# A recurrence over image columns: sigmoid of z into PSUM, running maximum by halves, and program order on every engine

## The chip, the cores and the metric

The kernel runs on one core of a Trainium2 chip. The core has a tensor engine (PE), a vector engine (VectorE, DVE in the profile), a scalar engine (ScalarE, ACT), GpSimd (POOL) and SyncE (SP), which here only issues DMA transfers. Each engine works through its own queue of instructions in order and waits on semaphores for the others. The metric is the device time of one execution in microseconds (us); lower is better. All data is float32.

## What is computed

The input x has shape (8, 32, 256, 256): batch, channel, row, column. Four layers follow one another, each as x + layer(groupnorm(x)): a Fourier layer, a 5x5 convolution, a recurrence over the columns, and a layer of running maxima in four directions with a 1x1 mix. The change touches the third layer. Cut to what matters, it is:

```python
def _cell(prev_col, cur_col, ...):          # both (batch, row, channel)
    x = concatenate([prev_col one row up, prev_col, prev_col one row down], axis=-1)
    i_vals = einsum('bhk,ok->bho', x, weight_ih) + bias_ih
    h_vals = einsum('bhc,oc->bho', cur_col, weight_hh) + bias_hh
    r = sigmoid(r_i + r_h); z = sigmoid(z_i + z_h)
    n = tanh(n_i + r * n_h)
    return n * z + cur_col * (1.0 - z)
# new_col of column w is prev_col of column w + 1; 255 such steps one after another
```

The fourth layer needs, among others, the running maximum of the third layer's result (with its residual added) from the first column to the last. That maximum is taken along the way, in the recurrence, since its columns come out in that order.

## The kernel before

The kernel has four stages: `forward_and_mix` and `inverse_and_conv` for the first two layers, `recurrence` for the third, `maxima_and_mix` for the fourth. They hand data on through DRAM: `x2d` into the recurrence, `x3d` (its result) and `fwd` (the running maximum) out of it.

In `recurrence` the 128 partitions are 4 residues of the row times 32 channels; the free axes are batch (8), column and 64 rows. Columns come in blocks of 8 (`WB`), 32 blocks (`NB`). Within a column the batch is worked on in two halves of 4 images (`NC`, index x), so that one half's matmuls can run while the other half's activations do. One step n = 2 w + x is one half of one column; a block has 16 steps. A step's tiles are 128 x 256.

One step consists of these parts (line numbers of before):

- `main` (L686): three matmuls of 128x128 weights for the gates r, z and ni, on the previous state `hs` of the same half.
- `cross` and `own` (both by L660): 32x32 matmuls, four at a time. `cross` adds the neighbours that `main` leaves out; `own` computes ahead for the NEXT step the part that depends on the current column alone (r, z and nh).
- L728: r = sigmoid on ScalarE. L729: VectorE (nh + bias) * r. L730: + ni.
- L731: z = sigmoid. L732: zm = 1 - z as a sigmoid of the negated value. L733: tanh.
- L735: GpSimd a = zm * current column. L737: VectorE n * z. L738: + a, which is the new state `hs`.
- L739: GpSimd adds the new state into the raw block `xw`, which becomes the layer's output.

Beside the steps there are: the load of a block from `x2d` (L645, 2 MB, four buffers), its normalisation on ScalarE (L653, eight activations of 128x512 a block into `xn`), the running maximum `fm` on VectorE (L763, one 128x512 per column, both halves at once), eight `bn_stats` a block (L775) for the next layer's statistics, and the stores of `x3d` and `fwd` (L752, eight transfers of 256 KB for each in every block).

The order in which an engine meets this work comes from two sources. Outside `manual_schedule` a scheduler orders instructions by their data and priorities; it may move a load far ahead. `keep_in_program_order` pins single instructions to where the code has them. The running maximum and the `bn_stats` are put in a list, and `late()` takes one of them in every step, between L730 and L737:

```python
                nc.gpsimd.tensor_tensor(a, zm, cur, ALU.mult)
                late()
                nc.vector.tensor_tensor(m, m, z, ALU.mult)
```

[...] Four tags for each half (r, z, ni, nh) take one bank each; [...]

Of the kernel before, what the change touches and what calls it, by code (L numbers as in the profile page):

```python
# [9 lines left out]
F32 = mybir.dt.float32  # L10
AF = mybir.ActivationFunctionType
ALU = mybir.AluOpType
# [4 lines left out]
P = 128  # L17
B, C, H, W = 8, 32, 256, 256
# [4 lines left out]
AFTER = mybir.DependencyInfo(mybir.DependencyClass.Sync, mybir.DependencyReason.DATA)  # L23
A = 4
Q = H // A
# [550 lines left out]
def recurrence(tc, k, d, x2d, x3d, fwd, stb, mean1, mv3):  # L576
# [4 lines left out]
    nc = tc.nc  # L581
    WB = 8
    NB = W // WB
    NH = 4
    NC = 2
    BC = B // NC
    with ExitStack() as ctx:
        one = ctx.enter_context(tc.tile_pool(name="bc", bufs=1))
        blk = ctx.enter_context(tc.tile_pool(name="bb", bufs=2))
        wk = ctx.enter_context(tc.tile_pool(name="bw", bufs=2))  # L590
        ps = ctx.enter_context(tc.tile_pool(name="bp", bufs=1, space=PSUM))

        def rows(i):
            return slice(32 * i, 32 * i + 32)
# [6 lines left out]
        for i in range(A):  # L601
            nc.sync.dma_start(out=wih[rows(i)], in_=d["wihT"].rearrange("(t c) (g o) -> c t g o", t=3, g=3))
            nc.sync.dma_start(out=whh[rows(i)], in_=d["whhT"].rearrange("c (g o) -> c g o", g=3))
            for j in range(A):
                if abs(i - j) < 2 and (i, j) not in ((1, 2), (2, 1)):
                    t = i - j + 1
                    nc.sync.dma_start(
                        out=wmain[rows(i), :, rows(j)],
# [3 lines left out]
        bhh = one.tile([P, 3], F32, name="bhh")  # L612
        nc.sync.dma_start(out=bih, in_=d["bih"])
        nc.sync.dma_start(out=bhh, in_=d["bhh"])
        brz = one.tile([P, 3], F32, name="brz")
# [23 lines left out]
        bst = one.tile([P, B, NB, 6], F32, name="bst")  # L639

        raws, norms, psums = {}, {}, {}

        def load(bi):
            t = blk.tile([P, B, WB, Q], F32, name=f"xw_{bi}", tag="xw", bufs=4)
            nc.sync.dma_start(  # L645
                out=t.rearrange("p b w q -> p b (w q)"),
                in_=x2d[:, :, :, bi * WB : (bi + 1) * WB, :].rearrange("b a c w q -> (a c) b (w q)"),
            )
            raws[bi] = t
            norms[bi] = blk.tile([P, B, WB, Q], F32, name=f"xn_{bi}", tag="xn")  # L650

        def normalise(bi, b):
            ins = nc.scalar.activation(  # L653
                norms[bi][:, b], raws[bi][:, b], AF.Identity, bias=shift[:, b : b + 1], scale=sc[:, 1, b : b + 1]
            )
            if bi:
                tc.keep_in_program_order(ins)

        def mm(out, i, j, lhsT, rhs, start, stop):
            return nc.tensor.matmul(out[rows(j)], lhsT=lhsT, rhs=rhs[rows(i)], start=start, stop=stop)  # L660

        R, Z, N = 0, 1, 2
# [4 lines left out]
        def own(n, gate):  # L667

            w, x = divmod(n, NC)
            if w >= W:  # L670
                return
            key = ("r", "z", "nh")[gate]
            out = psums[n, key] = ps.tile([P, BC, Q], F32, name=f"{key}_{n}", tag=f"{key}{x}")
            cur = norms[w // WB][:, x * BC : (x + 1) * BC, w % WB, :]
            for i in range(A):
                mm(out, i, i, whh[rows(i), gate, :], cur, True, gate == N)

        sem = tc.alloc_semaphore("own_parts")
        sigz = {}

        def main(n, prev):

            for gate, key in GATES:
                if gate == N:
                    psums[n, key] = ps.tile([P, BC, Q], F32, name=f"ni_{n}", tag=f"ni{n % NC}")
                nc.tensor.matmul(  # L686
                    psums[n, key], lhsT=wmain[:, gate, :], rhs=prev[:, :, 1 : 1 + Q], start=gate == N, stop=False
                )

        def cross(n, prev):  # L690

            for gate, key in GATES:
                if gate == Z:
                    own(n + 1, gate)
                for t, i, j, q0 in CROSS:
                    ins = mm(psums[n, key], i, j, wih[rows(i), t, gate, :], prev[:, :, q0 : q0 + Q], False, True)
                    if (gate, i) == (R, 3):
                        if n == NC:  # L700
                            ins._wait_ge(sem, 1)
                        else:
                            tc.add_manual_dep(ins.ins, sigz.pop(n - 1).ins.name, AFTER, reason="row groups of a bank")
                if gate != Z:
                    own(n + 1, gate)

        def step(w, x):
            bi, wi = w // WB, w % WB
            bs = slice(x * BC, (x + 1) * BC)
            raw, cur = raws[bi][:, bs, wi, :], norms[bi][:, bs, wi, :]  # L710
            new = hs[x][w % NH][:, :, 1 : 1 + Q]
            if w == 0:
                nc.vector.tensor_copy(new, cur)
            else:
                n, prev = NC * w + x, hs[x][(w - 1) % NH]
                if n == NC:
                    for gate in (R, Z, N):
                        own(n, gate)
                    tc.keep_in_program_order(nc.tensor.drain().then_inc(sem, 1))
                main(n, prev)  # L720
                cross(n, prev)
                p = {g: psums.pop((NC * w + x, g)) for g in ("r", "z", "ni", "nh")}
                r = wk.tile([P, BC, Q], F32, name=f"rs_{w}_{x}", tag=f"rs{x}")
                z = wk.tile([P, BC, Q], F32, name=f"zs_{w}_{x}", tag=f"zs{x}")
                m = wk.tile([P, BC, Q], F32, name=f"n_{w}_{x}", tag=f"n{x}")
                zm = wk.tile([P, BC, Q], F32, name=f"zm_{w}_{x}", tag=f"zm{x}")
                a = wk.tile([P, BC, Q], F32, name=f"a_{w}_{x}", tag=f"a{x}")
                nc.scalar.activation(r, p["r"], AF.Sigmoid, bias=brz[:, 0:1])  # L728
                nc.vector.scalar_tensor_tensor(m, p["nh"], bhh[:, 2:3], r, ALU.add, ALU.mult)  # L729
                nc.vector.tensor_tensor(m, p["ni"], m, ALU.add)  # L730
                sigz[n] = nc.scalar.activation(z, p["z"], AF.Sigmoid, bias=brz[:, 1:2])  # L731
                nc.scalar.activation(zm, p["z"], AF.Sigmoid, bias=brz[:, 2:3], scale=-1.0)  # L732
                nc.scalar.activation(m, m, AF.Tanh, bias=bih[:, 2:3])  # L733

                nc.gpsimd.tensor_tensor(a, zm, cur, ALU.mult)  # L735
                late()
                nc.vector.tensor_tensor(m, m, z, ALU.mult)  # L737
                nc.vector.tensor_tensor(new, m, a, ALU.add)  # L738
            nc.gpsimd.tensor_tensor(raw, raw, new, ALU.add)  # L739


        pieces, tops = [], {}

        def late():
            if pieces:
                tc.keep_in_program_order(pieces.pop(0)())

        def store(bi, dst, t):

            for a in range(A):  # L750
                for b2 in range(2):
                    nc.sync.dma_start(  # L752
                        out=dst[bi, :, b2, a].rearrange("(i c) n -> c i n", c=C),
                        in_=t[rows(a), 4 * b2 : 4 * b2 + 4].rearrange("p i w q -> p i (w q)"),
                    )

        def running(bi, wi):
            def piece():
                if wi == 0:
                    tops[bi] = blk.tile([P, B, WB, Q], F32, name=f"fm_{bi}", tag="fm", bufs=3)  # L760
                t, x = tops[bi], raws[bi][:, :, wi]
                last = t[:, :, wi - 1] if wi else tops[bi - 1][:, :, WB - 1] if bi else x
                ins = nc.vector.tensor_tensor(t[:, :, wi], x, last, ALU.max)  # L763
                if wi == WB - 1:
                    store(bi, fwd, t)
                return ins

            pieces.append(piece)

        def finish(bi):  # L770
            raw = raws[bi]
            store(bi, x3d, raw)
            for b in range(B):
                pieces.append(
                    lambda b=b: nc.vector.bn_stats(bst[:, b, bi, :], raw[:, b].rearrange("p w q -> p (w q)"))  # L775
                )

        load(0)
        for b in range(B):
            normalise(0, b)  # L780
        for bi in range(NB):
            if bi + 1 < NB:
                load(bi + 1)
            for wi in range(WB):
                for x in range(NC):
                    step(bi * WB + wi, x)
                running(bi, wi)
                if bi + 1 < NB and wi < WB // 2:
                    for b in (2 * wi, 2 * wi + 1):
                        normalise(bi + 1, b)  # L790
            finish(bi)
        while pieces:
            late()
        for b in range(B):
            nc.vector.bn_aggr(mv3[:, b, :], bst[:, b])

# [266 lines left out]
```

## Time and profile before

The time before is 3496.8 us, the median of 3 runs (3491.6 to 3498.0). The profiled execution spans 3489.2 us with a mean granted TensorE clock of 0.941.

| What | Value |
|---|---|
| PE busy | 3125.8 us, 90% of the span |
| VectorE busy | 2590.4 us, 74% |
| ScalarE busy | 1810.0 us, 52% |
| GpSimd busy | 883.8 us, 25% |
| L763 fm, 255 times | 289.7 us busy, mean 1136 ns |
| L739 raw add on GpSimd, 512 times | 349.8 us busy, mean 683 ns |
| L735 a on GpSimd, 510 times | 392.5 us busy, mean 770 ns |
| recurrence, 1262 to 2780 us | PE busy 1508.8 of 1518 us, VectorE 1286.7, ScalarE 1076.4, GpSimd 741.2 |
| DMA in that stretch | share 0.51, 130 GB/s |

In the groups of the page a row gives the line, engine and operation, the tiles written and read, the count, then the time busy in all and the mean of one, and last how long the engine was idle just before and who ended that wait. Busy time is an average over stages; what a change is worth in one stage is read from the waits of that stage. A busy PE isn't a PE at its peak.

### The profile page before, as it was taken

Reading aid. Unit: us, or ns where it says so; the run is one execution under the profiler, and the core shown is the slowest. Engines: PE = TensorE matmul, PEld = TensorE weight load, DVE = VectorE, ACT = ScalarE, POOL = GpSimd, SP = SyncE. Lnnn points to the kernel's source line nnn. Section 1 sums busy time; section 2 is a strip of 40 time slices with the busy share of each in tenths; the row PEclk is TensorE's granted clock in tenths of the full one; section 3 lists DMA queues with packets and bytes.
Section 4 is the critical chain, followed back from the end, with each engine's and each line's share of the span. In section 5 each row is a group of like instructions: output and inputs, shape, how many; then the busy total and the mean of one; then the engine's idle time right before and its main releaser. Section 6 shows DMA issues by size and latency. Waiting matters only on the chain.

```text
span 3489.2 us, 114177 instructions
## 1 busy us (share of the span) xinstructions
PE 3125.8 (90%) x48474; PEld 1700.8 (49%) x48474; DVE 2590.4 (74%) x5178; ACT 1810.0 (52%) x4098; POOL 883.8 (25%) x1211
## 2 busy tenths in 40 slices
PE   6776599999999969999999999999999867777787
PEld 4546244444444446666666666666666523232332
DVE  5553255556555548888888888888888889999998
ACT  3322255655665547777677777776777512222222
POOL 0010011111111025444444444454444400000000
PEclk9985699999999979999999999999999979999898
DMA  8887467777777445555455555545554377777775
GB/s 309 285 293 237 98 179 184 189 184 186 198 173 198 101 125 143 136 134 143 126 131 141 146 124 147 131 129 133 144 126 123 83 286 309 307 301 293 305 306 235
DMA packets 533869, 655.78 MB, mean 188 GB/s; under 512 B 394992, under 2 KB 395888, under 8 KB 507632
## 3 DMA queue, kind: packets, MB, share of 16 engines
q1 hardware_dynamic: 492272, 499.58, 50.9%
q0 software_dynamic: 15360, 79.70, 6.8%
q10 hardware_dynamic: 25728, 69.21, 5.0%
q8 instruction: 381, 6.24, 0.7%
q14 instruction: 128, 1.05, 0.1%
HBM read 371.54 MB, written 272.63 MB: 185 GB/s over the span
## 4 chain that ended last, share of the span: by engine, by line
PE 63%; DVE 22%; issue 4%; DMA 1%; SPq 1%; ACT 1%; POOL 0%; DVEq 0%; ACTq 0%; POOLq 0%
PE r L686 9%; PE r L660 8%; PE vp L446 7%; PE vp L454 7%; PE z L686 6%; PE ni L686 6%; PE z L660 6%; PE ni L660 5%; DVE rv L885 5%; PE up L405 4%; DVE dq L898 2%; DVE uq L899 2%; PE tp L388 2%; PE mp L258 1%; DVE top L896 1%
## 5 line engine op out<-in xcount | busy, mean ns | idle before, releaser
L739 POOL TENSOR_TENSOR xw<-xw,hs 128x256 f32<-128x256 f32 x512 | 349.8, 683 | 661.9 <-DVE hs L738 620.4
L936 ACT ACTIVATE ot<-o,bres 128x512 f32<-128x512 f32 x256 | 155.1, 688 | 551.6 <-PE o L920 545.0
L735 POOL TENSOR_TENSOR a<-zm,xn 128x256 f32<-128x256 f32 x510 | 392.5, 770 | 154.0 <-ACT zm L732 140.2
L728 ACT ACTIVATE rs<-r,brz 128x256 f32<-128x256 f32 x510 | 239.4, 469 | 286.0 <-PE r L660 285.8
L471 ACT ACTIVATE junk<-x 128x128 f32<-128x128 f32 (+1 forms) x384 | 202.8, 528 | 329.6 <-DVE x L465 323.5
L686 PE MATMUL r<-hs,wmain 128*128 128x256 f32 x1020 | 357.4, 432 | 1.9 <-DVE hs L738 1.2
L413 DVE TENSOR_TENSOR x<-up,xb 128x512 f32<-128x512 f32 x288 | 185.5, 686 | 227.6 <-PE up L405 217.6
L660 PE MATMUL r<-xn,whh 32*32 32x256 f32 x4080 | 323.8, 386 | 29.5 <-ACT xn L653 29.5
L729 DVE SCALAR_TENSOR_TENSOR n<-nh,bhh,rs 128x256 f32<-128x256 f32 x510 | 245.7, 482 | 114.0 <-ACT rs L728 114.0
L733 ACT ACTIVATE n<-n,bih 128x256 f32<-128x256 f32 x510 | 259.2, 508 | 132.2 <-DVE n L730 132.2
L660 PE MATMUL r<-hs,wih 32*32 32x256 f32 x4080 | 323.3, 386 | 0.0
L465 DVE SCALAR_TENSOR_TENSOR x<-vp,r,x 128x128 f32<-128x128 f32 (+2 forms) x512 | 236.8, 514 | 110.1 <-PE vp L454 109.9
L660 PE MATMUL ni<-hs,wih 32*32 32x256 f32 x4080 | 311.6, 373 | 2.6 <-issue 2.6
L660 PE MATMUL nh<-xn,whh 32*32 32x256 f32 x4080 | 312.5, 375 | 0.8 <-issue 0.8
L660 PE MATMUL z<-xn,whh 32*32 32x256 f32 x4080 | 311.8, 374 | 0.0
L660 PE MATMUL z<-hs,wih 32*32 32x256 f32 x4080 | 310.9, 373 | 0.3 <-issue 0.3
L686 PE MATMUL z<-hs,wmain 128*128 128x256 f32 x1020 | 303.8, 379 | 0.0
L686 PE MATMUL ni<-hs,wmain 128*128 128x256 f32 x1020 | 303.4, 379 | 0.0
L446 PE MATMUL vp<-x,c_conv 128*128 128x256 f32 (+2 forms) x768 | 290.0, 512 | 2.0 <-DVE x L465 2.0
L763 DVE TENSOR_TENSOR fm<-xw,fm 128x512 f32<-128x512 f32 x255 | 289.7, 1136 | 1.4 <-POOL xw L739 0.8
L920 PE MATMUL o<-dn,wsc 32*32 32x512 f32 x1536 | 208.4, 790 | 78.1 <-DVE dn L901 73.2
L454 PE MATMUL vp<-x,c_conv 64*64 64x256 f32 (+2 forms) x1536 | 277.7, 492 | 0.0
(160 smaller groups left out, 6277.0 us busy)
## 6 DMA issues: line engine op xcount, KB each, us to landing
xb<-in_xl_dram POOLq DMA_DIRECT2D x96, 768.0 KB, 6.0
xa<-in_xt_dram SPq DMA_DIRECT2D x64, 1024.0 KB
xw<-x2d SPq DMA_DIRECT2D x32, 2048.0 KB
x3d<-xw SPq DMA_DIRECT2D x256, 256.0 KB
fwd<-fm SPq DMA_DIRECT2D x256, 256.0 KB
x<-x3d SPq DMA_DIRECT2D x32, 2048.0 KB
fw<-fwd SPq DMA_DIRECT2D x32, 2048.0 KB
out_dram<-ot ACTq DMA_DIRECT2D x64, 1024.0 KB
```

Of the source, the lines that this page charges most:

```text
L446: nc.tensor.matmul(vp, lhsT=k.conv[:, 0:P], rhs=pair_of(u, ch, g, lo, hi), start=True, stop=False)
L454: nc.tensor.matmul(vp[o], lhsT=k.conv[r, P : P + 64], rhs=pair_of(u, ch, g, lo, hi, q0, r), start=False, stop=True,)
L465: nc.vector.scalar_tensor_tensor(x, src, state[u]["r"][ch][:, g : g + 1], x, ALU.mult, ALU.add, accum_out=s1[:, 0, n, ch, g : g + 1])
L660: return nc.tensor.matmul(out[rows(j)], lhsT=lhsT, rhs=rhs[rows(i)], start=start, stop=stop)
L686: nc.tensor.matmul(psums[n, key], lhsT=wmain[:, gate, :], rhs=prev[:, :, 1 : 1 + Q], start=gate == N, stop=False)
L728: nc.scalar.activation(r, p["r"], AF.Sigmoid, bias=brz[:, 0:1])
L729: nc.vector.scalar_tensor_tensor(m, p["nh"], bhh[:, 2:3], r, ALU.add, ALU.mult)
L733: nc.scalar.activation(m, m, AF.Tanh, bias=bih[:, 2:3])
L735: nc.gpsimd.tensor_tensor(a, zm, cur, ALU.mult)
L739: nc.gpsimd.tensor_tensor(raw, raw, new, ALU.add)
L763: ins = nc.vector.tensor_tensor(t[:, :, wi], x, last, ALU.max)
L920: nc.tensor.matmul(pts[b2][i][32 * j : 32 * j + 32].rearrange("p (w q) -> p w q", q=Q), lhsT=wsc[q, b2, t, :], rhs=src[j][q, b2], start=first,
```

## The change

Four things are changed in `recurrence`, and nothing outside it:

1. z = sigmoid is written into PSUM instead of SBUF, into the free half of the nh bank. nh's tile is now 128 x 2 x 256: the matmuls write the first half, ScalarE writes z in the second. [...] z waits for VectorE's (nh + bias) * r, and it comes behind zm instead of ahead of it. VectorE's n * z then reads one operand from SBUF and one from PSUM.
2. The running maximum is taken by halves (128x256) and directly: that of step n - 1 stands on VectorE behind the new state of step n. The list keeps only `bn_stats`, at the same place as before.
3. The normalisation of the next block moves from the first four columns of a block (two at a time) to its third to sixth (one in every step).
4. The whole loop stands in `manual_schedule(engines=None)`: every engine, SyncE's queue of transfers too, gets its instructions in the order of the code. The calls to `keep_in_program_order` go.

It is meant to keep the running maximum and GpSimd's work out of each other's way, off the path from one state to the next, and to have the order on every engine fixed by the code.

```diff
         def normalise(bi, b):
-            ins = nc.scalar.activation(
+            nc.scalar.activation(
                 norms[bi][:, b], raws[bi][:, b], AF.Identity, bias=shift[:, b : b + 1], scale=sc[:, 1, b : b + 1]
             )
-            if bi:
-                tc.keep_in_program_order(ins)
...
-            out = psums[n, key] = ps.tile([P, BC, Q], F32, name=f"{key}_{n}", tag=f"{key}{x}")
+            if gate == N:
+
+                psums[n, "nh"] = ps.tile([P, 2, BC, Q], F32, name=f"nh_{n}", tag=f"nh{x}")
+                out = psums[n, "nh"][:, 0]
+            else:
+                out = psums[n, key] = ps.tile([P, BC, Q], F32, name=f"{key}_{n}", tag=f"{key}{x}")
...
-                    tc.keep_in_program_order(nc.tensor.drain().then_inc(sem, 1))
+                    nc.tensor.drain().then_inc(sem, 1)
...
-                z = wk.tile([P, BC, Q], F32, name=f"zs_{w}_{x}", tag=f"zs{x}")
...
+                nh, z = p["nh"][:, 0], p["nh"][:, 1]
                 nc.scalar.activation(r, p["r"], AF.Sigmoid, bias=brz[:, 0:1])
-                nc.vector.scalar_tensor_tensor(m, p["nh"], bhh[:, 2:3], r, ALU.add, ALU.mult)
+                nhr = nc.vector.scalar_tensor_tensor(m, nh, bhh[:, 2:3], r, ALU.add, ALU.mult)
+                sigz[n] = nc.scalar.activation(zm, p["z"], AF.Sigmoid, bias=brz[:, 2:3], scale=-1.0)
+                ins = nc.scalar.activation(z, p["z"], AF.Sigmoid, bias=brz[:, 1:2])
+                tc.add_manual_dep(ins.ins, nhr.ins.name, AFTER, reason="one engine in a bank at a time")
                 nc.vector.tensor_tensor(m, p["ni"], m, ALU.add)
-                sigz[n] = nc.scalar.activation(z, p["z"], AF.Sigmoid, bias=brz[:, 1:2])
-                nc.scalar.activation(zm, p["z"], AF.Sigmoid, bias=brz[:, 2:3], scale=-1.0)
                 nc.scalar.activation(m, m, AF.Tanh, bias=bih[:, 2:3])
 
                 nc.gpsimd.tensor_tensor(a, zm, cur, ALU.mult)
-                late()
+                if pieces:
+                    pieces.pop(0)()
...
+        def running(n):
+
+            w, x = divmod(n, NC)
+            bi, wi = w // WB, w % WB
+            bs = slice(x * BC, (x + 1) * BC)
...
+            t, v = tops[bi], raws[bi][:, bs, wi]
+            last = t[:, bs, wi - 1] if wi else tops[bi - 1][:, bs, WB - 1] if bi else v
+            nc.vector.tensor_tensor(t[:, bs, wi], v, last, ALU.max)
+            if (wi, x) == (WB - 1, NC - 1):
+                store(bi, fwd, t)
...
-        for bi in range(NB):
-            if bi + 1 < NB:
-                load(bi + 1)
-            for wi in range(WB):
-                for x in range(NC):
-                    step(bi * WB + wi, x)
-                running(bi, wi)
-                if bi + 1 < NB and wi < WB // 2:
-                    for b in (2 * wi, 2 * wi + 1):
-                        normalise(bi + 1, b)
-            finish(bi)
...
+        with tc.manual_schedule(engines=None):
+            load(0)
             for b in range(B):
...
+                normalise(0, b)
+            for bi in range(NB):
+                if bi + 1 < NB:
+                    load(bi + 1)
+                for wi in range(WB):
+                    for x in range(NC):
+                        n = (bi * WB + wi) * NC + x
+                        step(bi * WB + wi, x)
+                        if n:
+                            running(n - 1)
+                        if bi + 1 < NB and 2 <= wi < 2 + WB // 2:
+                            normalise(bi + 1, 2 * (wi - 2) + x)
+                store(bi, x3d, raws[bi])
```

More of the change, by code (lines that the diff above doesn't have):

```diff
@@ L742, in recurrence @@
         pieces, tops = [], {}
-        def late():
-            if pieces:
-                tc.keep_in_program_order(pieces.pop(0)())
         def store(bi, dst, t):
@@ L755, in store @@
                     )
[L757 to L768, printed above, removed]
@@ L770, in finish @@
-        def finish(bi):
-            raw = raws[bi]
-            store(bi, x3d, raw)
-            for b in range(B):
[L774 to L780, printed above, removed]
-        for bi in range(NB):
-            if bi + 1 < NB:
-                load(bi + 1)
-            for wi in range(WB):
-                for x in range(NC):
-                    step(bi * WB + wi, x)
-                running(bi, wi)
-                if bi + 1 < NB and wi < WB // 2:
-                    for b in (2 * wi, 2 * wi + 1):
-                        normalise(bi + 1, b)
-            finish(bi)
@@ L792, in recurrence @@
-        while pieces:
-            late()
+        def running(n):
+            w, x = divmod(n, NC)
+            bi, wi = w // WB, w % WB
+            bs = slice(x * BC, (x + 1) * BC)
+            if (wi, x) == (0, 0):
+                tops[bi] = blk.tile([P, B, WB, Q], F32, name=f"fm_{bi}", tag="fm", bufs=3)
+            t, v = tops[bi], raws[bi][:, bs, wi]
[3 more added lines that the diff above has]
+                store(bi, fwd, t)
+                raw = raws[bi]
+                for b in range(B):
+                    pieces.append(
+                        lambda b=b: nc.vector.bn_stats(bst[:, b, bi, :], raw[:, b].rearrange("p w q -> p (w q)"))
+                    )
@@ new lines, in recurrence @@
+        with tc.manual_schedule(engines=None):
+            load(0)
+            for b in range(B):
+                normalise(0, b)
[11 more added lines that the diff above has]
+                store(bi, x3d, raws[bi])
+            running(NC * W - 1)
+            for piece in pieces:
+                piece()
```

## The prediction

> **What bounds the kernel now.** I read the page's slices first (the recurrence is the stretch from 1262 to 2780 us, 1518 of 3489 us, PE 9 tenths or more throughout), then the chain, then single steps in the timeline, then the SyncE queue and the DMA share by windows. The chain of the page and three of its groups:
>
> ```profile
> PE 63%; DVE 22%; issue 4%; DMA 1%; SPq 1%; ACT 1%; POOL 0%; DVEq 0%; ACTq 0%; POOLq 0%
> ...
> L739 POOL TENSOR_TENSOR xw<-xw,hs 128x256 f32<-128x256 f32 x512 | 349.8, 683 | 661.9 <-DVE hs L738 620.4
> ...
> L763 DVE TENSOR_TENSOR fm<-xw,fm 128x512 f32<-128x512 f32 x255 | 289.7, 1136 | 1.4 <-POOL xw L739 0.8
> ```
>
> PE leads, though the running maximum (fm) looks dear: 1136 ns on average. Is PE really the limit, or does it wait for the new state hs? Timeline, columns: start us, length us, engine, line, what:
>
> ```profile
> 2022.92 0.70 PE L686 MATMUL r<-hs,wmain 128*128 128x256 f32 x2
> ...
> 2024.89 0.42 DVE L738 TENSOR_TENSOR hs<-n,a 128x256 f32<-128x256 f32 x1
> ...
> 2025.86 0.70 PE L686 MATMUL r<-hs,wmain 128*128 128x256 f32 x2
> ...
> 2028.25 0.43 DVE L738 TENSOR_TENSOR hs<-n,a 128x256 f32<-128x256 f32 x1
> ...
> 2028.81 0.70 PE L686 MATMUL r<-hs,wmain 128*128 128x256 f32 x2
> ```
>
> The first matmul of a step comes every 2.947 us. At 2025.86 its hs had been done for 0.55 us (2024.89 + 0.42), at 2028.81 for 0.13 us, and the spacing is the same: PE sets the pace itself. 509 spacings of 2.947 are 1500 us of the 1511 us between first and last; at most 11 us can be won in the loop.
>
> A step in the other half of a block, where fm runs:
>
> ```profile
> 2005.67 0.42 DVE L730 TENSOR_TENSOR n<-ni,n 128x256 f32<-128x256 f32 x1
> ...
> 2005.98 0.73 POOL L735 TENSOR_TENSOR a<-zm,xn 128x256 f32<-128x256 f32 x1
> ...
> 2006.01 1.25 DVE L763 TENSOR_TENSOR fm<-xw,fm 128x512 f32<-128x512 f32 x1
> 2006.13 0.51 ACT L733 ACTIVATE n<-n,bih 128x256 f32<-128x256 f32 x1 [0.23 <-DVE n L730]
> ...
> 2007.18 0.41 DVE L737 TENSOR_TENSOR n<-n,zs 128x256 f32<-128x256 f32 x1
> ```
>
> fm takes 1.25 because GpSimd's L735 began 0.03 earlier; it ends 0.55 after L735. It holds back L737, which could follow the tanh at 6.64. But hs still meets PE's next start with 0.06 to spare: the change attacks a wait that PE does not feel.
>
> Then the loads. SyncE's queue and who waited for the block load (L645):
>
> ```profile
> 1998.30 0.38 SPq L645 DMA_DIRECT2D xw<-x2d  x1
> 2017.75 8.36 SPq L752 DMA_DIRECT2D x3d<-xw  x8
> 2026.21 8.99 SPq L752 DMA_DIRECT2D fwd<-fm  x8
> 2045.45 0.38 SPq L645 DMA_DIRECT2D xw<-x2d  x1
> ```
> ```profile
> who waited for it (us, times):
>   ACT xn L653: 37.2, 1
> ```
>
> One wait only, for the very first load: the load at 2045.45 is for a block normalised two blocks later (the queue holds four loads ahead of the first store).
>
> [...] fm is 0.68 where it starts first (some 40 times; L735 then takes 1.26), 1.24 where GpSimd does. [...] The trace has one case: after an idle of 1.84 us at 2435.14 the matmuls of r take 1.22 instead of 0.70, and that step 4.21 instead of 2.95.
>
> **The change, part by part.** (1) fm becomes halves of 128x256 behind hs: 510 x 0.42 (as L738, also two SBUF inputs) for 255 x 1.14. It starts about 0.08 before L738 ends, GpSimd's add 0.08 after, [...] GpSimd waits 0.26, with 1.5 us idle there. (2) [...] ScalarE now does z behind L729, which ends 0.59 + 0.46 - 0.48 = 0.57 before the tanh starts, and z takes 0.47: hidden. (3) The own nh matmul must now wait for L737 of the step before: in PE's time that ends 1.8 us after the step's first matmul, nh comes at 2.4: hidden. (4) bn_stats, 0.68, lies under the tanh as before. VectorE's whole step: L729 to L738 0.59 + 0.46 + 0.54 + 0.53 = 2.12, L738 to fm 0.34, fm to the next L729 0.34: 2.80, under 2.947. So parts 1 to 4 leave PE's pace alone: nothing, at best the first steps' 2 us.
>
> (5) Program order on all engines. In the changed kernel as built, SyncE has: load(0), load(1), and then for each block eight x3d stores of the block before, load of the NEXT block, eight fwd stores. The load can't be issued before the last of the x3d stores, which wait for GpSimd's last raw add (L744). And ScalarE has the first normalise of that load behind the tanh of the block's fifth step, by a wait on the DMA. What time is there? Count from the first matmul of the last step of a block, by the rows above: r's sigmoid at 2.26, L729 2.76, L738 4.88, hs 5.30, fm to 5.64, raw add to 6.32. The normalise stands at 5 x 2.947 + 3.81 (tanh) + 0.41 = 18.95. Between: 12.6 us. The next sigmoid of r is due at 6 x 2.947 + 2.26 = 19.94 and the normalise takes 0.70 ahead of it: 0.3 spare; the loop has 0.5 more (hs at 5.30, wanted at 5.83). So 13.4 us are free.
>
> What is needed: in before, the second halves' add ends at 2020.67 and the last six stores are through the queue at 2026.11: 5.4 us, 1.28 each once the queue is full; now seven wait for it: 6.4 (5.9 to 6.7). Then the load: alone, with no stores ahead, the first takes from 1246.50 to 1256.15, 9.65 us; the one at 2045.45 shows DMA shares of 0.93 to 2051 and 0.68 to 2055, the same. Behind stores still in the rings it takes 0 to 3 us more; I take 1. Sum 6.4 + 9.6 + 1 = 17.0, bounds 15.6 and 19. Late by 17.0 - 13.4 = 3.6 us a block (2.2 to 5.6). Queued behind the normalise: r, z and tanh of the sixth step, so L729 to L738 behind them, and PE's r cross matmuls of the seventh (they wait for sigmoid of z), then all. PE is idle over 3 us then, so its clock may halve: in a step by step reckoning with these rows 0 or 0.9 more; I take 0.9. 4.5 us a block, 30 blocks (load(1) is early, the last block loads none): +135. Less 2: 3496.8 + 133 = 3630.
>
> **The rivals.**
> - Load in time, PE's pace kept: the sums of parts 1 to 4 speak for it, the 15.6 against 13.4 against it. It would need a load of under 7 us; the second of the four queued at the start landed some 5.5 behind the first, so not absurd. 3494.
> - Faster: VectorE's freed time reaches PE. Against it, 2.947 us also where hs is 0.55 early. All irregular steps gone would give 3486; below 3489.8 needs that nearly whole.
> - VectorE becomes the bound: [...] fm takes 0.56 more: 2.80 + 0.56 = 3.36 a step, 0.41 x 510 = +210, the load then less late (five steps give 2 us): +40; 3750. Against it, the 0.16 us by which fm starts earlier.
>
> **How the numbers follow.** Late loads 0.85: with 2.2 a block and the clock kept 3561, with 5.6 + 0.9 3690. A little more room for a load of 15 us and a longer queue: 3540 to 3700, which holds 0.80. In time 0.06, faster 0.03, [...] Faster 0.03, same 0.06, slower 0.91.
>
> **What would show it.** Right: in the profile after, normalise (L653) is 30 times idle before with a DMA as releaser, some 4 to 6 us each; the load is issued 6 us after the last raw add; fm 0.42; median step still 2.947, one step in 16 long; PE clock low behind it. Wrong: no idle at normalise [...]; fm near 1.0 [...]; a median step other than 2.947 (VectorE or PE's new wait for L737 bounds).

## The result, and the profile after

The changed kernel takes **3706.5 us** (median; 3703.1 to 3715.0), the kernel before 3494.2 (3480.9 to 3498.0) on the same chip: a ratio of 1.062, 95% interval 1.058 to 1.065. The forecast was 3630, with a range up to 3700; the result lies above it. Direction and cause were as forecast; the loss, 212 us, is larger than the 133 forecast.

The chain of the page after, to be set beside that of before. The transfer of the block load is on it with 11%, where it was not among the lines of before, and PE falls from 63% to 50%:

```profile
PE 50%; DVE 21%; DMA 13%; issue 4%; ACT 2%; SPq 2%; POOL 1%; DVEq 0%; ACTq 0%; POOLq 0%
DMA xw<-x2d 11%; PE r L658 6%; PE vp L446 6%; PE r L689 6%; PE vp L454 6%; PE z L658 4%; DVE rv L886 4%; PE z L689 4%; PE ni L689 4%; PE ni L658 4%; PE up L405 4%; DVE dq L899 2%; DVE uq L900 2%; PE tp L388 2%; PE mp L258 1%
```

Three groups of the page after: GpSimd's raw add (0.68 us before, 0.80 now), the cross matmuls of r, the normalisation (mean ns, then idle time before and its releaser):

```profile
L744 POOL TENSOR_TENSOR xw<-xw,hs 128x256 f32<-128x256 f32 x512 | 411.4, 804 | 719.5 <-DVE hs L743 679.6
L658 PE MATMUL r<-hs,wih 32*32 32x256 f32 x4080 | 336.5, 400 | 170.6 <-ACT zm L733 170.6
...
L653 ACT ACTIVATE xn<-xw,shift,sc 128x512 f32<-128x512 f32 x256 | 204.2, 800 | 253.7 <-DMA xw<-x2d 253.7
```

The view of the normalisation's own instructions says how often it waited. In before it waited once, for 37.2 us; now:

```profile
its engine sat idle before it (us, times) until:
  DMA xw<-x2d: 253.7, 31
```

The first wait is again that for the first load (37.4). The other 30 are 216.3 us, 7.2 for each block.

One block end in the timeline of after (start, length, engine, line). The running maximum is short now, 0.42 after hs. SyncE is what to look at: seven x3d stores wait for the raw add, then come the load and the fwd stores:

```profile
1415.65 0.42 DVE L743 TENSOR_TENSOR hs<-n,a 128x256 f32<-128x256 f32 x1
...
1415.99 0.42 DVE L767 TENSOR_TENSOR fm<-xw,fm 128x256 f32<-128x256 f32 x1
...
1416.15 0.80 POOL L744 TENSOR_TENSOR xw<-xw,hs 128x256 f32<-128x256 f32 x1 [1.32 <-DVE hs L743]
...
1416.98 7.24 SPq L753 DMA_DIRECT2D x3d<-xw  x7
...
1424.32 1.24 SPq L645 DMA_DIRECT2D xw<-x2d  x1
...
1425.65 12.27 SPq L753 DMA_DIRECT2D fwd<-fm  x8
```

Raw add done at 1416.95, load issued at 1424.32, landed at 1437.6. The same block 13 us later, timeline of after:

```profile
1429.32 0.51 ACT L737 ACTIVATE n<-n,bih 128x256 f32<-128x256 f32 x1
...
1437.62 0.81 ACT L653 ACTIVATE xn<-xw,shift,sc 128x512 f32<-128x512 f32 x1 [7.80 <-DMA xw<-x2d]
1438.34 0.45 ACT L731 ACTIVATE rs<-r,brz 128x256 f32<-128x256 f32 x1
...
1439.21 0.65 PE L658 MATMUL r<-hs,wih 32*32 32x256 f32 x4 [6.25 <-ACT zm L733]
```

ScalarE has finished the fifth step's tanh and stands 7.80 us in front of the normalisation, with the sigmoids of the sixth step behind it; PE, in the seventh step, runs dry 6.25 us for the sixth step's L733, the sigmoid of the negated z. When it starts again a cross matmul takes 0.65 instead of 0.39 to 0.42. Five of the 2 us windows of that stretch (PE, PEld, VectorE, ScalarE, GpSimd busy; then PE clock, DMA share, GB/s) say why:

```profile
1431.00:1433.00 2.00, 1.96 (x28) 1.05 (x6) 0.14 (x1) 0.00 (x0) 0.68 (x1) 1.00 0.95 326
1433.00:1435.00 2.00, 0.00 (x0) 0.00 (x0) 0.00 (x0) 0.00 (x0) 0.00 (x0) 1.00 1.04 376
1435.00:1437.00 2.00, 0.00 (x0) 0.00 (x0) 0.00 (x0) 0.00 (x0) 0.00 (x0) 0.64 1.05 388
...
1439.00:1441.00 2.00, 1.79 (x40) 0.93 (x48) 1.79 (x5) 1.73 (x5) 0.73 (x1) 0.50 0.69 231
1441.00:1443.00 2.00, 2.00 (x28) 1.11 (x17) 1.90 (x5) 1.63 (x5) 1.49 (x2) 0.66 0.13 51
```

The granted clock falls while PE waits (a mean of 0.64 over 1435 to 1437) and is 0.50 when it starts (1439 to 1441); the DMA share is full (1.04 and 1.05 from 1433 to 1437), so the transfer is running and not held up by a wait.

Over the recurrence, the spacings of the steps' first matmuls give the whole account. The median is 2.947 us in both kernels. Above 509 times that, after has 227.6 us, of which 211.4 are in the spacing that begins with the seventh step of a block and 15.4 in the next: 226.8 / 30 = 7.56 us a block. Before has 10.9 us, in a few irregular steps. 227.6 - 10.9 = 216.7, and the profiled spans differ by 3707.0 - 3489.2 = 217.8. What else has moved comes to 1 us in the sum.

### The profile page after: what moved, and what is told of

Same layout as the page of the kernel before. It is cut to its first block, busy times and chain, and to the rows that moved or that the text cites. A ratio compares the mean times of both kernels' runs of the same rounds, so it can differ in the third digit from the quotient of the medians.

```text
span 3707.0 us, 114348 instructions
## 1 busy us (share of the span) xinstructions
PE 3177.2 (86%) x48474; PEld 1716.4 (46%) x48474; DVE 2512.5 (68%) x5434; ACT 1870.3 (50%) x4098; POOL 923.4 (25%) x1211
## 4 chain that ended last, share of the span: by engine, by line
PE 50%; DVE 21%; DMA 13%; issue 4%; ACT 2%; SPq 2%; POOL 1%; DVEq 0%; ACTq 0%; POOLq 0%
DMA xw<-x2d 11%; PE r L658 6%; PE vp L446 6%; PE r L689 6%; PE vp L454 6%; PE z L658 4%; DVE rv L886 4%; PE z L689 4%; PE ni L689 4%; PE ni L658 4%; PE up L405 4%; DVE dq L899 2%; DVE uq L900 2%; PE tp L388 2%; PE mp L258 1%
## 5 line engine op out<-in xcount | busy, mean ns | idle before, releaser
L744 POOL TENSOR_TENSOR xw<-xw,hs 128x256 f32<-128x256 f32 x512 | 411.4, 804 | 719.5 <-DVE hs L743 679.6
L658 PE MATMUL r<-hs,wih 32*32 32x256 f32 x4080 | 336.5, 400 | 170.6 <-ACT zm L733 170.6
L739 POOL TENSOR_TENSOR a<-zm,xn 128x256 f32<-128x256 f32 x510 | 371.7, 729 | 273.8 <-ACT zm L733 238.8
L732 DVE SCALAR_TENSOR_TENSOR n<-nh,bhh,rs 128x256 f32<-128x256 f32 x510 | 246.5, 483 | 265.8 <-ACT rs L731 240.1
L658 PE MATMUL r<-xn,whh 32*32 32x256 f32 x4080 | 337.0, 401 | 29.8 <-ACT xn L653 29.8
L653 ACT ACTIVATE xn<-xw,shift,sc 128x512 f32<-128x512 f32 x256 | 204.2, 800 | 253.7 <-DMA xw<-x2d 253.7
L658 PE MATMUL nh<-xn,whh 32*32 32x256 f32 x4080 | 325.5, 390 | 0.0
L658 PE MATMUL z<-xn,whh 32*32 32x256 f32 x4080 | 325.5, 389 | 0.0
L658 PE MATMUL z<-hs,wih 32*32 32x256 f32 x4080 | 324.5, 388 | 0.0
L658 PE MATMUL ni<-hs,wih 32*32 32x256 f32 x4080 | 324.5, 388 | 0.0
L742 DVE TENSOR_TENSOR n<-n,nh 128x256 f32<-128x256 f32 x510 | 215.1, 422 | 150.6 <-ACT n L737 150.6
```

Of the source, the lines that this page charges most:

```text
L653: nc.scalar.activation(norms[bi][:, b], raws[bi][:, b], AF.Identity, bias=shift[:, b : b + 1], scale=sc[:, 1, b : b + 1])
L732: nhr = nc.vector.scalar_tensor_tensor(m, nh, bhh[:, 2:3], r, ALU.add, ALU.mult)
```

## The experiments

### Is the late load the whole loss?

Theory: ScalarE's wait for the load costs all of it. Rival: some comes from parts 1 to 3, or from all engines being held to the order of the code. If the load is late, its lateness has two possible sources, which the later experiments part: the fwd stores issued right behind it share its bandwidth, or the x3d stores issued right ahead of it are still being moved (2a and 2b, where the expectations number them; B and A in that of e5). Two edits take the wait away, one from either side.

**e1** leaves every transfer as it is, and normalises three steps later:

```diff
-                        if bi + 1 < NB and 2 <= wi < 2 + WB // 2:
-                            normalise(bi + 1, 2 * (wi - 2) + x)
+                        if bi + 1 < NB and 7 <= 2 * wi + x < 15:
+                            normalise(bi + 1, 2 * wi + x - 7)
```

> The changed kernel with one edit: the eight normalisations of the next block stand behind steps 7 to 14 of a block (0 to 15) instead of 4 to 11, which is 8.8 us later. The order of transfers is untouched. Theory 1 (the whole loss is the normalise waiting for a late load, about 7.3 us in each of 30 blocks): the wait is gone or under 1 us, 3490 to 3500 us. Rival (program order also costs elsewhere, through VectorE's fm, z behind nh*r or the nh matmul's new wait): the time stays well above before, 3530 or more, with a median step above 2.947 us.

**e2** leaves the normalisation and puts the load ahead of the x3d stores of the block before:

```diff
                 if bi + 1 < NB:
                     load(bi + 1)
+                if bi:
+                    store(bi - 1, x3d, raws[bi - 1])
...
-                store(bi, x3d, raws[bi])
+            store(NB - 1, x3d, raws[NB - 1])
```

> The changed kernel with one edit: in SyncE's queue the load of the next block stands ahead of the eight x3d stores of the block before, so it can be issued about a block earlier. Normalisations stay at steps 4 to 11. Theory 1: no wait for the load is left, 3485 to 3495 us; the load alone lands 9.5 to 12 us after its issue, as in the kernel before. Rival (it is the place of the normalisations, or something else in program order): no better than 3600.

Measured: e1 3494.8 (ratio to before 1.0011, 1.0003 to 1.0020), e2 3495.9 (1.0022, 1.0013 to 1.0031), before 3489.4 on that chip. The waits of the normalisation in e1:

```profile
  DMA xw<-x2d: 37.1, 2
```

The first load's wait is left (37.0), and one of 0.17. In e1 the load still lands 13.1 us behind its issue, as late as in the changed kernel, but nobody asks for it so early. So that wait is all but 5 or 6 us of the loss: with z in PSUM, fm by halves and program order all in place, either edit brings the time back to 0.1 or 0.2% above before. Both intervals exclude 1, and e2 came 0.9 above its forecast (its load took 12.7 us, where 9.5 to 12 was expected; a table below shows what stood ahead of it); this small rest is taken up under e6. Neither is faster than before, so parts 1 to 4 gain nothing here.

### Why is the load so slow: what stands ahead of it, or behind?

**e3** moves the fwd stores in the code behind the fourteenth step of the next block:

```diff
-                store(bi, fwd, t)
+                waiting.append((bi, t))
...
+                        if (wi, x) == (WB - 2, NC - 1) and waiting:
+                            b0, t0 = waiting.pop()
+                            store(b0, fwd, t0)
```

> The changed kernel with one edit: the eight fwd stores of a block are issued ten steps later (behind step 13 of the next block), so no transfer stands right behind the load; the eight x3d stores still stand ahead of it. It tells apart why the load took 13.3 us instead of the 10.6 of the prediction. Theory 2a (transfers issued behind the load share the DMA engines with it): the load lands 2 to 3 us sooner, the normalise waits 4 to 5 us instead of 7.2, about 3630 us. Theory 2b ([...] only the x3d stores ahead delay the load): nothing changes, about 3706 us.

Measured: 3716.0, ratio 1.0652 (1.0636 to 1.0668), idle 257.5 us in 31 waits: as the changed kernel. It is inconclusive, since the edit did not do what it was meant to. SyncE has only transfers in its queue. Moving a store behind other engines' work in the code leaves SyncE's own order (x3d, load, fwd) alone, and nothing makes it wait: the fwd stores were again issued 1.3 us behind the load. Program order is an order on each engine, not a time.

**e4** puts one x3d store ahead of the load and seven behind it, with the eight fwd stores after those (`store` now takes a slice of its eight transfers, and takes the second half of the batch first, so that the one ahead still waits for the last raw add):

```diff
+                if bi:
+                    store(bi - 1, x3d, raws[bi - 1], slice(1, None))
...
-                store(bi, x3d, raws[bi])
+                store(bi, x3d, raws[bi], slice(0, 1))
```

> The changed kernel with one edit: of the eight x3d stores only one (a second half, which waits for the same last raw add) stands ahead of the load, seven stand right behind it, then fwd. The load is issued about 0.4 us after the last raw add instead of 7.4. Theory 1 with 7 us less to wait for: if stores behind it slow the load (2a) it still lands some 13 us after issue, 13.5 in all against 13.4 free, so a wait of 0 to 1 us and 3490 to 3520 us. Theory 2b: landing after 10 us, no wait, 3490 us.

**e5** does what e3 meant: the first fwd store waits for the new state of the tenth step of the next block.

```diff
-                store(bi, fwd, t)
+                waiting.append((bi, t))
...
+                        if (wi, x) == (4, 1) and waiting:
+                            store(waiting[0][0], fwd, waiting.pop()[1], news[n])
...
+                    if gate is not None and (a, b2) == (0, 0):
+                        tc.add_manual_dep(ins.ins, gate.ins.name, AFTER, reason="stores late in the block")
```

> The changed kernel with one edit: the first fwd store of a block waits for the new state of the tenth step of the next block, so that nothing stands behind the load on SyncE until about 29 us into the block; the x3d stores still stand ahead of it. Theory A (the transfers that are in flight AHEAD of the load stretch it): it still lands about 13 us behind its issue, 7 us of idle a block at the first normalise, about 3700 us. Rival B (the eight fwd stores issued BEHIND it share its bandwidth): it lands 10.3 us behind its issue, as the lone load of the kernel before; idle 4.5 us a block, about 3630 us.

Measured: e4 3504.0 (1.0044, 1.0029 to 1.0059), no wait at the normalisation but the first; its load landed after 11.3 us, between the 10 and the 13 of the two theories. e5 3714.5 (1.0644, 1.0622 to 1.0666), against before 3489.8. SyncE's queue and a ScalarE row of the timeline of e5, in the same block:

```profile
1368.12 9.62 SPq L753 DMA_DIRECT2D x3d<-xw  x8
1377.78 1.30 SPq L645 DMA_DIRECT2D xw<-x2d  x1
1407.07 8.09 SPq L753 DMA_DIRECT2D fwd<-fm  x8
...
1391.25 0.81 ACT L653 ACTIVATE xn<-xw,shift,sc 128x512 f32<-128x512 f32 x1 [7.34 <-DMA xw<-x2d]
```

For 28 us nothing stands behind the load, and it is as late as ever: issued at 1377.78, used at 1391.25. The time from a load's issue to the last of its completions in the trace, over the blocks behind the first four, by what stands about it:

| Kernel | Right ahead on SyncE | Right behind | Issue to landing, median us (10th to 90th in a hundred) |
|---|---|---|---|
| e6 (below) | nothing for some 8 us | nothing | 10.1 (9.7 to 11.3) |
| before | nothing for some 10 us | nothing | 10.4 (9.6 to 11.3) |
| e4 | one x3d store | 15 stores | 11.3 (10.8 to 12.1) |
| e2 | eight fwd stores | nothing for 27 us | 12.7 (11.9 to 13.8) |
| changed kernel | eight x3d stores | eight fwd stores | 13.1 (12.6 to 13.8) |
| e5 | eight x3d stores | nothing for 28 us | 13.2 (12.8 to 13.9) |

So it is what stands ahead: eight stores ahead cost 2.3 to 3.1 us more than none, fifteen behind (with one ahead) about 1. The prediction's order, the load behind the stores that are still being moved, was its author's estimate; these times agree with it.

The packets of the DMA engines in the traces say how much was left. Between a load's issue and its landing, SyncE's transfers moved 2.10 MB in the median of before and of e6, which is the load alone, but 2.65 MB in e5 and 2.66 in e2. So about 0.55 MB, two stores of 256 KB, was still to be moved when SyncE turned to the load. At e5's 203 GB/s that takes 2.7 us, and the load was 2.8 us later than in before. In the changed kernel 3.68 MB went through in 13.1 us: a further MB, of the fwd stores behind, was moved in the same time at 281 GB/s in all.

### Do parts 1 to 4 shorten anything, and does PE hide it?

The prediction had VectorE's step at 2.80 us, under PE's 2.947. If that is so, a lighter PE should bring the gain out. First pair: **p1** is the kernel before and **p2** is e2, both with ni's four cross matmuls left out of every step.

```diff
-                for t, i, j, q0 in CROSS:
+                for t, i, j, q0 in CROSS if gate != N else ():
```

> The kernel before, with the ni gate's four cross matmuls of 32x32 left out of every step (the neighbours' part of ni is not computed, so the result is not the reference's). It takes work off PE alone. If PE sets the pace of a step: the spacing falls from 2.947 to about 2.73 in the steps without fm and to 2.9 or 3.0 in those with the long fm, [...]: about 40 us less, 3455. If VectorE (or the way from one state to the next) sets the pace: 3489, unchanged.

> The changed kernel with the load ahead of the x3d stores (no late load) and the same four cross matmuls of ni left out. If fm by halves and z in PSUM do take 0.3 to 0.6 us from VectorE's path in the steps with fm, and PE merely hides it: every step goes at about 2.80 (VectorE's sum in the prediction), no long ones, about 75 us less than 3490: 3415, and below the kernel before with the same matmuls left out. If they bring nothing even then: the same as that kernel, about 3455, or more.

Measured: p1 3487.4 (0.9987, 0.9975 to 0.9998), p2 3483.8 (0.9986, 0.9978 to 0.9994). Both miss: the median step is 2.947 in both. By the expectation's words this speaks against PE as the bound. The timelines of before and of p1 show that the experiment, not the reading, was off. First before, then p1:

```profile
2022.35 0.39 PE L660 MATMUL ni<-hs,wih 32*32 32x256 f32 x4
2022.38 0.39 PE L660 MATMUL nh<-xn,whh 32*32 32x256 f32 x4
```
```profile
2021.63 0.39 PE L660 MATMUL z<-hs,wih 32*32 32x256 f32 x4
2021.65 0.39 PE L660 MATMUL z<-xn,whh 32*32 32x256 f32 x4
2021.87 0.61 PE L660 MATMUL nh<-xn,whh 32*32 32x256 f32 x8
2022.41 0.70 PE L686 MATMUL r<-hs,wmain 128*128 128x256 f32 x2
```

In p1, z's cross (on hs) and own matmuls (on xn) start 0.02 us apart and take 0.39 each: in the trace they overlap. So did those of ni and nh in before, 0.03 apart, and the own matmuls of nh alone take the place that both took: from the last z group to the next step's first matmul it is 0.78 us in p1 (2022.41 - 2021.63) and 0.79 in before (2022.92 - 2022.13). Nothing was taken off PE's time. The unmoved step of 2.947 us puts a price on it: four such matmuls, twice over, beside four others cost nothing here.

Second pair, with work that stands alone on PE: ni's 128x128 matmul left out, in **p3** from the kernel before, in **p4** from e6 below.

```diff
             for gate, key in GATES:
...
+                if gate == N:
+                    continue
```

> The kernel before with the ni gate's 128x128 matmul left out of every step (the neighbours that it covers are missing from ni, so the result is not the reference's). Leaving out ni's cross matmuls moved nothing, since nh's own four run beside them on the array; this one stands alone on PE, 0.43 us from z's to the first cross matmul. If PE's chain sets the pace: the steps with bn_stats go at about 2.52 us, those with fm stay near 2.9, where VectorE (0.48 + 0.42 + 1.25 + 0.41 + 0.43 = 2.99 busy) takes over: about 110 us less, 3380. If something else sets 2.947 (VectorE's loop, ScalarE): 3489, unchanged.

> The changed kernel with the load two blocks ahead and the same matmul of ni left out of every step. If parts 1 to 4 do shorten VectorE's work and PE merely hides it: steps with bn_stats near 2.84 (0.48 + 0.42 + 0.68 + 0.41 + 0.43 + 0.42), those without near PE's 2.52, on average 2.68: about 135 us less, 3355, and 25 us less than the kernel before with the same matmul left out. If parts 1 to 4 bring nothing even where PE has room: the same as that kernel, about 3380, or more.

Measured: p3 3460.6 (0.9915, 0.9900 to 0.9930), p4 3414.7 (0.9790, 0.9773 to 0.9807), before 3490.1. Both sizes were missed (3380 and 3355), but the step does move, as it should if PE set it. It could also move because ni's matmul lies on the way from one state to the next; against that stands the page's row of before, where PE sat idle 1.9 us ahead of all the steps' first matmuls together, 1.2 of them for the state hs:

```profile
L686 PE MATMUL r<-hs,wmain 128*128 128x256 f32 x1020 | 357.4, 432 | 1.9 <-DVE hs L738 1.2
```

In p3 that idle time is 153 us. The two kernels differ by 46 us where 25 were expected. VectorE in the timeline of p3, in a step with fm:

```profile
2030.99 0.48 DVE L731 SCALAR_TENSOR_TENSOR n<-nh,bhh,rs 128x256 f32<-128x256 f32 x1
...
2031.57 0.42 DVE L732 TENSOR_TENSOR n<-ni,n 128x256 f32<-128x256 f32 x1
...
2031.97 1.10 DVE L765 TENSOR_TENSOR fm<-xw,fm 128x512 f32<-128x512 f32 x1
...
2032.99 0.41 DVE L739 TENSOR_TENSOR n<-n,zs 128x256 f32<-128x256 f32 x1
...
2033.51 0.42 DVE L740 TENSOR_TENSOR hs<-n,a 128x256 f32<-128x256 f32 x1
...
2033.85 0.48 DVE L731 SCALAR_TENSOR_TENSOR n<-nh,bhh,rs 128x256 f32<-128x256 f32 x1
```

And the same view of p4:

```profile
2010.58 0.47 DVE L735 SCALAR_TENSOR_TENSOR n<-nh,bhh,rs 128x256 f32<-128x256 f32 x1
2011.16 0.42 DVE L739 TENSOR_TENSOR n<-ni,n 128x256 f32<-128x256 f32 x1
2012.16 0.42 DVE L745 TENSOR_TENSOR n<-n,nh 128x256 f32<-128x256 f32 x1 [0.57 <-ACT n L740]
2012.69 0.42 DVE L746 TENSOR_TENSOR hs<-n,a 128x256 f32<-128x256 f32 x1
2013.03 0.42 DVE L770 TENSOR_TENSOR fm<-xw,fm 128x256 f32<-128x256 f32 x1
2013.37 0.48 DVE L735 SCALAR_TENSOR_TENSOR n<-nh,bhh,rs 128x256 f32<-128x256 f32 x1
```

In p3 VectorE goes from one instruction to the next without idling: 2033.85 - 2030.99 = 2.86, and from + ni to n * z it takes 1.42 with fm between. In p4 that stretch takes 1.00, 0.57 of it a wait for the tanh, and fm adds 0.34 behind hs. The loop closes in 2.79, and the median step is 2.785, in steps with and without bn_stats. That is the prediction's 2.80.

In the half of a block where p3 normalises, its steps alternate between 2.52 and 3.30, mean 2.91. The timeline of p3 shows why:

```profile
2009.19 1.50 ACT L653 ACTIVATE xn<-xw,shift,sc 128x512 f32<-128x512 f32 x2
...
2010.60 0.45 ACT L730 ACTIVATE rs<-r,brz 128x256 f32<-128x256 f32 x1
...
2011.09 0.49 DVE L731 SCALAR_TENSOR_TENSOR n<-nh,bhh,rs 128x256 f32<-128x256 f32 x1 [0.82 <-ACT rs L730]
```

Two normalisations stand together on ScalarE ahead of the sigmoid of r, and VectorE waits 0.82 us for it in every second step. In p4, which takes one in every step (part 3 of the change), those steps go at 2.79 too. So the gain of parts 1 to 4 is real: 0.08 us a step in the half where p3 takes fm (from fm by halves and z in PSUM, not told apart) and 0.12 in the half where it normalises (there part 3 ends the long steps). In the kernel as it is, PE's 2.947 hides all of it. The expectations were too low: that of p3 left out the pairs of normalisations, that of p4 let PE set the steps without bn_stats, where VectorE's loop does.

### A version that keeps the order and loses nothing

**e6** loads two blocks ahead (the `xn` tile is now taken at its first normalisation), in front of the x3d stores:

```diff
+            load(1)
...
-                if bi + 1 < NB:
-                    load(bi + 1)
+                if bi + 2 < NB:
+                    load(bi + 2)
+                if bi:
+                    store(bi - 1, x3d, raws[bi - 1])
```

> The changed kernel with the load two blocks ahead (load of block bi + 2 at the start of block bi, in front of the x3d stores; everything else in its order, nothing left out). Theory: the load has a whole block more, normalise never waits; a step of 2.947 throughout, parts 1 to 4 bring nothing that PE lets through: 3485 to 3496 us, the same as before. Rival: with the load out of the way the shorter path of VectorE shows, 3475 or less. Second rival: the irregular steps come from the order of the code itself (all engines in program order) and stay: 3500 or more.

Measured: 3489.0 against 3489.8, ratio 0.9992 (0.9982 to 1.0002): the same as before, as the first theory had it. The normalisation's waits in e6:

```profile
  DMA xw<-x2d: 37.1, 1
```

Its irregular steps, those above the median, sum to 5.5 us (before 10.9, e1 14.4, e2 15.4, e4 20.8). In e4 the groups put some 11 us of idle time of PE down to "issue". The irregular steps fell to 3.0 us in p1 and 1.6 in p2, which have eight fewer matmul instructions a step. What PE waits for there stays open; the differences of up to 0.4% between e1, e2, e4, e6 and before are of about that size. No version that computes the whole result was clearly faster than the kernel before.

## Why the prediction was wrong in size

Point by point, by its own steps:

- **PE sets the pace**: right. The median step stayed at 2.947; with PE 0.43 us lighter it fell to 2.86 (p3).
- **Parts (1) to (4) give nothing**: right. fm took 0.42, GpSimd's add took 0.12 longer (0.80 against 0.68; a wait of 0.26 was forecast). z behind L732, nh's wait for n * z and bn_stats left the step alone (e1, e2, e6). n * z, which in before took 0.41 to 0.95 us (over 0.85 in 41 of 510 steps), took 0.40 to 0.42 with z in PSUM. VectorE's step of 2.80 was 2.785 where PE let it show (p4). Nothing came of them because PE hid it, as the prediction said.
- **SyncE's order, the place of the wait, and what is queued behind it**: right. 30 waits at L653, ahead of the sixth step's sigmoids, PE then dry in the seventh step for L733.
- **The 6.4 us to the load's issue**: somewhat low. The median is 6.9 (6.8 to 7.7), over its bound of 6.7.
- **The load, 9.6 alone and 1 more behind stores**: this is the step that failed. "Behind stores still in the rings it takes 0 to 3 us more; I take 1." That was an estimate for which before had no row: there each load came some 10 us behind the last store. It took 13.1 instead of 10.6. Of these 2.5 us, 1.7 are the stores ahead, 2.7 instead of 1, which e5 shows by itself (2.8). The other 0.8 are the lone load: 9.65 was the first one, and the median of before's is 10.4. The prediction took the load at 2045.45 for the same 9.65 from its DMA shares; by its completions it landed after 11.4.
- **Late by need less 13.4**: the main part of the free time was nearly right, 12.9 from the raw add to the end of the tanh (median) where 12.6 was forecast. Need 20.0 (median; 17.0 forecast), so 6.6 late instead of 3.6. With the prediction's estimate of 0.9 for the halved clock, 7.5 a block; measured 7.56. So the 0.9 fits as what is left over; no run measured the clock's part by itself.
- **30 blocks, less 2**: 30 x 7.56 = 227; 10 of before's 10.9 us of irregular steps went instead of 2, why is open. 227 - 10 = 217, near the 217.8 of the spans; by the medians it is 212.

So the miss is nearly all one sum: 3 us a block in issue and load, 30 times, less the 8 us at the end, which came in the prediction's favour by luck. The stores' part lay inside its bounds of 0 to 3, near the top, where 1 was taken; the issue and the lone load came out above what they had been given, so that the sum passed its upper bound of 19. The range ended at 5.6 + 0.9 a block and a little more.

Of the rivals, "in time" fell with the 30 waits, "faster" with e6, and VectorE as the bound (fm at 0.98, a longer median step) with fm at 0.42.

## What to carry to other kernels

When a load is put behind stores in one engine's queue of transfers, count its latency from the last store's own wait and measure it behind stores, not from a lone load; here the same 2 MB took 13.1 us instead of 10.4, and the issue came 7 us late on top. Where an engine normalises, copies or converts the loaded block early, in strict order with latency-bound work, look for each late microsecond in the whole kernel's time: here ScalarE waited 216.3 us in all, and the span grew by 217.8. Move the load a block further ahead, or its first use a few steps later. And before shortening one engine's loop, take some work off the engine that sets the pace and see how much of the gain appears: it was 46 us here with PE lighter, and nothing without.

## What the runs showed of the hardware

- A load of 2 MB behind eight stores of 256 KB landed 12.7 to 13.2 us after its issue, against 10.1 to 10.4 with none ahead; fifteen stores behind it (and one ahead) made it only 11.3. What was left of the stores ahead was some 0.55 MB (e5, e2).
- In the block shown, PE's granted clock fell to 0.50 about 2.6 us after PE ran dry (dry from 1432.96; a mean of 0.64 over 1435 to 1437 puts the fall at 1435.56), and was full again some 3.1 us after it restarted at 1439.21 (a mean of 0.66 over 1441 to 1443 puts the rise at 1442.4). The fall came 2.1 to 3.8 us after PE ran dry in 29 of the 30 blocks and 5.4 in the first; the clock stayed low for 6.83 us in 28 blocks, and for 3.41 and 10.24 in one each. In before PE was idle for 1.84 us ahead of 2435.14, and the clock was 0.50 from 2436 to 2438.
- Leaving out four 32x32 matmuls, twice over in each of the 510 steps, that start 0.02 to 0.03 us from four others left the step at 2.947 us (p1, p2).
